# Degree one-hots as whole-block bf16 operations in a graph and mixture-of-experts layer

## The chip, the cores and the metric

One Trainium2 chip, one of its cores. The metric is the device time of one execution, in microseconds (us). PE is TensorE (PEld its weight loads), DVE is VectorE, ACT is ScalarE, POOL is GpSimd, SP is SyncE, which here only starts transfers.

## The reference, cut to what matters

One layer over 6250 nodes of 256 numbers and 100,000 edges sorted by target. It has a graph convolution, a linear attention and a mixture of 16 experts, two per node. The part around the change is the degree of each node, its inverse root, and the normalised rows that the edges gather:

```python
def gcn_residual(x, edge_index, edge_weight, W, b, gamma, beta):
    src, dst = (edge_index[0], edge_index[1])
    h = x @ W
    deg = jax.ops.segment_sum(edge_weight, dst, num_segments=N_NODES) + 1.0
    dinv = jax.lax.rsqrt(deg)
    norm = dinv[src] * edge_weight * dinv[dst]
    agg = jax.ops.segment_sum(norm[:, None] * h[src], dst, num_segments=N_NODES)
    agg = agg + (dinv * dinv)[:, None] * h
...
xn = _layernorm(x, axis=-1)
x = x + gcn(xn, edge_index, edge_weight, ...) + mix(xn[None], ...)[0]
x = x + ffn(_layernorm(x, axis=-1)[None], ...)[0]
```

## The kernel before

**Stages.** `gps_layer` loads the edges' targets, weights and sources as rows of 1024 (`load_rows`: targets by SP's queue, weights and sources by ACT's), and X, the nodes' rows, by SP's queue. It turns the edges' rows into columns of 128 edges by PE's transposes (`columns`, L158 to L165): `loc_t` (the target within the window of the edge's chunk), `w_t`, `src_t`. A check that the edges fit into these windows decides between two layers; `windowed_layer` is the one that runs, and all that follows is in it.

**The degree stage** (L397 to L520). There are NCH = 782 chunks of 128 edges, each with a window of 128 nodes. The degrees come from products of one-hots. A target within its window is split into its low four bits `lo_b` and its high bits `hi_b` (HI = 8 values). The weight is split into three bf16 parts (`thirds`, `w3`), whose sum has the precision of f32. DVE goes through blocks of 98, 98, 196, 196 and 196 chunks. For a block it builds `lo1`, the one-hot of the low bits, with 16 operations (L460), and `hw`, the one-hot of the high bits times each of the three weight parts, with 24 (L464). PE then makes one product per chunk (L472): 128 edges, 16 low values by 24 columns (8 high values times 3 parts), added into PSUM at the chunk's group. PSUM holds three banks, each of HB = 168 groups of three columns; a product that crosses the edge of a bank is split in two. Products with zeros open and close each bank (L454, L480). Both one-hots have two buffers, so DVE may be up to two blocks ahead of PE.

When the banks are closed, DVE adds the three parts (L506). PE spreads the 16 x groups onto partitions with eight products against `spread` (L514). ACT takes the root (L517), and DVE the reciprocal `dinv` and its product with the layer norm's inverse deviation (L518 to L520). `keep_pace` (L484) is a row of products with zeros that nobody reads.

**Beside it.** ACT sums the first SA = 32 tiles of X and their squares (`two_sums`, L441), in groups of eight; DVE takes the statistics of the other 17 with bn_stats (L498). `constants` and the splitting of two bias rows (L490, L492) also run on DVE. SP's queue loads the weights and then writes zeros over the first 88 of 129 blocks of `xslots`, the experts' input rows in device memory (`fill`, L385, eight blocks or 1 MB for each transfer; SOON = 88, L394).

**The table.** DVE and ACT write `hs`, each node's row normalised and scaled by `dinv` (`table`, L529), in groups of seven tiles that SP's queue stores (L540). `table` is called from the first 14 slots of the main loop, numbered -14 to -1.

**The main loop** (L1358) runs over slots, about one for each chunk. The order of PE, DVE, ACT and SP is written out by hand: each engine runs its instructions in the order in which the program makes them. In a slot POOL starts the gather of a chunk's 128 rows of `hs` (L1364), DVE builds the chunk's weighted one-hot (L1369), and PE multiplies (L1377). `Weave` runs pieces of other work at slots that are set beforehand: the attention (`attend`), the residual, the routing, POOL's scatter of tokens to `xslots` (L1040), the experts, whose results go to `yslots`. ACT's queue writes the rest of the zeros from slot 4 on, one transfer every eight slots, first `yslots`, then the rest of `xslots` (L1280). `own_term` (L660) loads a tile's own row of `hs` into a ring of ten buffers (`ring`, L652). The tail then gathers the experts' results (L1180) and ends the layer.

The lines L558 to L567 (half of `par`, the mask `heads`, the ones in `xa`) stand on DVE between the degree stage and the table.

Of the kernel before, what the change touches and what calls it, by code (L numbers as in the profile page):

```python
# [111 lines left out]
HB = 168  # L112
# [17 lines left out]

WA = 2 * F
# [13 lines left out]
def evicted_at(c):  # L145

    return product_at(c) + (3 if c < 16 * PHASES[-2] else 1)

# [39 lines left out]
def gps_layer(ctx: ExitStack, tc: tile.TileContext, x, src, dst, ew, **rest):  # L188
# [12 lines left out]
    flag = top.tile([1, 1], I32, name="flag")  # L201
    with tc.tile_pool(name="chk", bufs=1) as cp, \
# [4 lines left out]
        v.memset(dst_e[:, PADC:], N - 1)  # L207
        v.memset(ew_e[:, PADC:], 0.0)
# [37 lines left out]
    with tc.If(ok) as cmp:  # L246
        windowed_layer(tc, X, ident, loc_t, w_t, src_t, **rest)
# [11 lines left out]
def windowed_layer(ctx: ExitStack, tc: tile.TileContext, X, ident, loc_t, w_t, src_t, W, b, gamma, beta, wqT, wkvT, wprojT, bproj,  # L259
# [124 lines left out]

    def fill(eng, a, first, end):  # L385

        zero = zero_b.bitcast(F32)
        for s in range(first, end, 8):
            q = min(8, end - s)
            eng.dma_start(a[s * P:(s + q) * P, :].rearrange("(p q) c -> p q c", q=q),  # L390
                          zero[:, None, :].to_broadcast([P, q, D]))
            yield 8

    SOON = 88  # L394
    for _ in fill(nc.sync, xslots, 0, SOON):
        pass
    with tc.tile_pool(name="deg", bufs=1) as sp, \  # L397
            tc.tile_pool(name="deg_ps", bufs=1, space=bass.MemoryType.PSUM) as sps:
        spread = sp.tile([16, 8, P], F32, name="spread")
        nc.gpsimd.memset(spread, 0.0)  # L400
        for a in range(8):
            nc.gpsimd.tensor_copy(spread[:, a, a * 16:(a + 1) * 16], ident[:16, :16])

        rowf = sp.tile([1, NB3], F32, name="rowf")
        nc.scalar.dma_start(rowf[:, :D], b.rearrange("(p c) -> p c", p=1))
        nc.scalar.dma_start(rowf[:, D:2 * D], bproj.rearrange("(p c) -> p c", p=1))
# [3 lines left out]
        nc.scalar.dma_start(b2f, experts.rearrange("(e p) w -> e p w", p=P)[:, 0, WROW - D:])  # L410
        b2s = sp.tile([NE, 3, D], BF, name="b2s")

        loc_i = sp.tile([P, NCA], I16, name="loc_i")
        v.tensor_copy(loc_i, loc_t)
        lo_i = sp.tile([P, NCA], I16, name="lo_i")
        hi_i = sp.tile([P, NCA], I16, name="hi_i")
        v.tensor_scalar(lo_i, loc_i, 15, None, op0=OP.bitwise_and)
        v.tensor_scalar(hi_i, loc_i, 4, None, op0=OP.logical_shift_right)
        lo_b = sp.tile([P, NCA], BF, name="lo_b")
        hi_b = sp.tile([P, NCA], BF, name="hi_b")  # L420
# [3 lines left out]
        def thirds(o, a):  # L424
            left = sp.tile([P, NCA], F32, name="left", bufs=2)[:a.shape[0], :a.shape[1]]
            v.tensor_copy(o[:, 0, :], a)
            v.tensor_sub(left, a, o[:, 0, :])
            v.tensor_copy(o[:, 1, :], left)
            v.tensor_sub(left, left, o[:, 1, :])
            v.tensor_copy(o[:, 2, :], left)  # L430

        w3 = sp.tile([P, 3, NCA], BF, name="w3")
        thirds(w3, w_t)


        SA = 32
# [4 lines left out]
        def two_sums():  # L441
            for t0 in range(0, SA, 8):
                for t in range(t0, t0 + 8):
                    act(sp.tile([P, D], F32, name="unread", bufs=2), X[:, t, :], AF.Identity,
                        accum_out=sums_[:, t:t + 1])
                act(minus[:, t0:t0 + 8], sums_[:, t0:t0 + 8], AF.Identity, scale=-1.0 / D)
                for t in range(t0, t0 + 8):
                    act(sp.tile([P, D], F32, name="unread", bufs=2), X[:, t, :], AF.Square,
                        bias=minus[:, t:t + 1], accum_out=squares[:, t:t + 1])


        deg = sps.tile([16, 3, 512], F32, name="deg")
        for i in range(3):
            nc.tensor.matmul(deg[:, i, :3 * HB], zero_b[:, :16], zero_b[:, :3 * HB], start=True, stop=False)  # L454
        C = NCA // 4
        c0 = 0
        for n in (C // 2, C // 2, C, C, C):
            lo1 = sp.tile([P, 16, C], BF, name="lo1", bufs=2)
            for i in range(16):
                v.tensor_scalar(lo1[:, i, :n], lo_b[:, c0:c0 + n], float(i), None, op0=OP.is_equal)  # L460
            hw = sp.tile([P, HI, 3, C], BF, name="hw", bufs=2)
            for i in range(HI):
                for s in range(3):
                    v.scalar_tensor_tensor(hw[:, i, s, :n], hi_b[:, c0:c0 + n], float(i), w3[:, s, c0:c0 + n],  # L464
                                           op0=OP.is_equal, op1=OP.mult)
            for c in range(c0, min(c0 + n, NCH)):
                g0 = 4 * group_of(c)
                h0 = g0
                while h0 < g0 + HI:
                    i = h0 // HB  # L470
                    h1 = min(g0 + HI, (i + 1) * HB)
                    nc.tensor.matmul(deg[:, i, (h0 - i * HB) * 3:(h1 - i * HB) * 3], lo1[:, :, c - c0],  # L472
                                     hw[:, h0 - g0:h1 - g0, :, c - c0].rearrange("p h s -> p (h s)"),
                                     start=False, stop=False)
                    h0 = h1
            if c0 == 0:
                two_sums()
            c0 += n
        for i in range(3):
            nc.tensor.matmul(deg[:, i, :3 * HB], zero_b[:, :16], zero_b[:, :3 * HB], start=False, stop=True)  # L480

# [8 lines left out]
        thirds(row3, rowf)  # L490
        nc.sync.dma_start(bias3, row3)
        thirds(b2s, b2f)  # L492
# [8 lines left out]
        v.bn_aggr(mv1[:rows(NFULL), NFULL, :], halves[NFULL][:rows(NFULL)])  # L501
        v.tensor_scalar(mv1[:, :SA, 0], minus, -1.0, None, op0=OP.mult)
        v.tensor_scalar(mv1[:, :SA, 1], squares, 1.0 / D, None, op0=OP.mult)
        deg16 = sp.tile([16, 3, HB], F32, name="deg16")
        for i in range(3):
            v.tensor_reduce(deg16[:, i, :], deg[:, i, :3 * HB].rearrange("p (h s) -> p h s", s=3),  # L506
                            axis=AX.X, op=OP.add)
        inv_std(sp, rs1, mv1[:, :, 1])
        minus_mean(nm1, mv1, rs1)

        dps = sps.tile([P, NT], F32, name="dps")
        d8 = deg16.rearrange("p i h -> p (i h)")[:, 4:4 + 8 * NT].rearrange("p (t a) -> p t a", a=8)
        for a in range(8):
            nc.tensor.matmul(dps, spread[:, a, :], d8[:, :, a], start=(a == 0), stop=(a == 7))  # L514
        keep_pace(10)
        sdeg = sp.tile([P, NT], F32, name="sdeg")
        act(sdeg, dps, AF.Sqrt, bias=ones[:, 0:1], scale=1.0)  # L517
        v.reciprocal(dinv, sdeg)  # L518
# [39 lines left out]
    v.tensor_scalar(par, par, 0.5, None, op0=OP.mult)  # L558
    heads = part(P)
    v.memset(heads, 0.0)  # L560
    for h in range(P // HEAD):
        v.memset(heads[h * HEAD:(h + 1) * HEAD, h * HEAD:(h + 1) * HEAD], 1.0)
    XA = 6
    xa = []
    for i in range(XA):
        xa.append(part(D + 1))
        v.memset(xa[i][:, D:], 1.0)  # L567
# [82 lines left out]
    RING = 10  # L650
    hTs = [wp.tile([P, F], F32, name=f"hT{j}") for j in range(2)]
    ring = [wp.tile([P, D], F32, name=f"agg{j}") for j in range(RING)]  # L652
# [627 lines left out]
    for a, first in (yslots, 0), (xslots, SOON):  # L1280
# [77 lines left out]
    while slot <= evicted_at(NCH - 1) or weave.steps:  # L1358
        for t in range(NT * (slot + PRE) // PRE, NT * (slot + PRE + 1) // PRE if slot < 0 else 0):
            table(t)  # L1360
# [554 lines left out]
```

## Time and profile before

| | us |
|---|---|
| median of 11 runs | 1465.18 |
| lowest and highest run | 1461.02, 1468.98 |
| the profiled execution | 1470.76 |
| its span, first to last instruction | 1469.0 |
| first one-hot of the degree stage | 21.09 |
| last bank closed | 71.42 |
| table begins | 79.72 |
| first gather | 106.81 |
| last gather issued | 1206.70 |

The profile is one execution, taken by the hardware profiler. The page gives each engine's busy time and share of the span, and groups of instructions: source line, engine, operation, output<-input by the program's names, shape, count, busy us, mean ns of one, then the idle time of the engine just before them and what ended it. A timeline lists instructions in order of time: start, length, engine, line, and in brackets the idle time before and who ended it. Matmuls are pipelined and their ends are modelled, so the distance between starts says more than a single length. An f32 matmul shows as two records. The granted clock is the share of TensorE's full speed that the throttle left, 0.931 over the whole span. Busy shares of the span are PE 83%, PEld 67%, POOL 65%, DVE 62%, ACT 34%.

### The profile page before, as it was taken

What the parts mean: (1) busy time and instruction counts of PE and PEld (TensorE: products, weight loads), DVE (VectorE), ACT (ScalarE), POOL (GpSimd) and SP (SyncE); (2) the same over time, 40 slices, a digit from 0 to 9 for tenths busy, and PEclk for the clock granted to TensorE, in tenths of its full rate; (3) what the DMA queues carried; (4) which work ended last, traced back from release to release, by engine and by line L of the source; (5) the groups of instructions that cost most, each with busy time, mean ns of one, the idle gap of its engine ahead of it and who ended that gap; (6) DMA issues with size and microseconds to landing.
All of it is one profiled execution on the core that took longest, in us unless ns stands there. A gap on an engine that the chain in (4) does not pass through costs nothing. (4 is left out here: it accounts for less than half of the span.)

```text
span 1469.0 us, 24398 instructions
## 1 busy us (share of the span) xinstructions
PE 1216.7 (83%) x6927; PEld 989.0 (67%) x6927; DVE 914.5 (62%) x3303; ACT 501.4 (34%) x1428; POOL 962.1 (65%) x998
## 2 busy tenths in 40 slices
PE   4889999978837897989968899797986999878880
PEld 3846666656625786868857787586875887767670
DVE  7954444449958583855837568286582657657764
ACT  6464444412202221322322223132231233446772
POOL 1007777777777777777777777777777763157732
PEclk9999999989967998989989999898998999989995
DMA  8976666763334777877868877687877886899983
GB/s 260 312 236 219 188 216 206 223 216 105 104 118 163 247 229 227 273 260 246 278 203 297 268 230 270 220 280 245 278 249 263 308 300 206 296 332 388 383 298 86
DMA packets 180593, 357.20 MB, mean 243 GB/s; under 512 B 27157, under 2 KB 119692, under 8 KB 180442
## 3 DMA queue, kind: packets, MB, share of 16 engines
q1 hardware_dynamic: 110334, 204.18, 40.4%
q0 software_dynamic: 47712, 128.17, 27.8%
q10 hardware_dynamic: 22396, 23.10, 4.8%
q8 instruction: 61, 1.00, 0.3%
q14 instruction: 90, 0.74, 0.2%
HBM read 279.28 MB, written 76.06 MB: 242 GB/s over the span
## 5 line engine op out<-in xcount | busy, mean ns | idle before, releaser
L1364 POOL DMA_INDIRECT hrow<-w_hs,src_t x782 | 758.6, 970 | 325.1 <-issue 88.1
L1377 PE MATMUL acc<-hrow,hot 128*128 128x256 f32 x1564 | 448.4, 405 | 105.0 <-DMA hrow<-w_hs,src_t 94.4
L1377 PEld LDWEIGHTS acc<-hrow,hot 128*128 128x128 f32 x1564 | 282.4, 200 | 182.7 <-issue 89.4
L1369 DVE TENSOR_SCALAR hot<-iota_g,loc_t,w_t 128x128 f32<-128x128 f32 x782 | 247.2, 354 | 65.3 <-PE acc L1377 64.4
L1129 ACT ACTIVATE hT<-hp,early 128x128 f32<-128x128 f32 x292 | 83.2, 369 | 256.0 <-PE hp L1122 134.1
L1133 PE MATMUL yp<-early,hT 128*128 128x256 f32 x584 | 143.8, 391 | 0.4 <-ACT hT L1129 0.4
L1122 PE MATMUL hp<-Q,early 128*128 128x128 f32 x992 | 124.5, 280 | 3.9 <-ACT Q L1116 3.9
L1122 PEld LDWEIGHTS hp<-Q,early 128*128 128x128 f32 x992 | 122.7, 197 | 7.4 <-ACT Q L1116 4.9
L1133 PEld LDWEIGHTS yp<-early,hT 128*128 128x128 f32 x584 | 114.2, 198 | 16.9 <-ACT hT L1129 0.5
L1040 POOL DMA_INDIRECT w_xslots<-Q,slot_i x92 | 91.6, 996 | 40.2 <-issue 32.0
L1122 PE MATMUL hp<-Q 128*128 128x128 f32 x832 | 104.8, 280 | 12.1 <-ACT Q L1116 12.0
L1122 PEld LDWEIGHTS hp<-Q 128*128 128x128 f32 x832 | 102.3, 196 | 15.8 <-ACT Q L1116 13.8
L1386 DVE SCALAR_TENSOR_TENSOR agg<-acc,dinv,agg 64x256 f32<-64x256 f32 x135 | 65.1, 482 | 70.5 <-PE acc L1377 68.0
L588 PE MATMUL kq<-early,xnT 128*128 128x512 f32 (+1 forms) x196 | 94.3, 604 | 6.3 <-ACT xnT L584 6.3
L1133 PE MATMUL yp<-Q,hT 128*128 128x256 f32 x328 | 86.1, 409 | 5.0 <-ACT hT L1129 5.0
L596 DVE SCALAR_TENSOR_TENSOR row<-two_a,two_b 128x256 f32<-128x256 f32 (+1 forms) x49 | 20.9, 426 | 103.4 <-ACT two_b L593 103.4
L1180 POOL DMA_INDIRECT late<-w_yslots,slot_i x48 | 48.6, 1012 | 49.6 <-DVE xn L1208 20.0
L1129 ACT ACTIVATE hT<-hp,Q 128x128 f32<-128x128 f32 x164 | 46.7, 370 | 93.7 <-issue 44.1
L1133 PEld LDWEIGHTS yp<-Q,hT 128*128 128x128 f32 x328 | 66.5, 208 | 16.3 <-ACT hT L1129 6.2
L1180 POOL DMA_INDIRECT agg<-w_yslots,slot_i x50 | 50.7, 1013 | 22.5 <-DVE xn L1195 6.3
L1111 PE MATMUL xtp<-ident,Q 128*128 128x128 f32 x228 | 46.2, 285 | 22.9 <-DMA Q<-w_xslots 21.5
L1116 ACT COPY Q<-xtp 128x256 f32<-128x256 f32 x114 | 43.1, 378 | 54.9 <-PE xtp L1111 54.6
(322 smaller groups left out, 1765.5 us busy)
## 6 DMA issues: line engine op xcount, KB each, us to landing
early<-in_experts SPq DMA_DIRECT2D x60, 642.0 KB
early<-in_experts SPq DMA_DIRECT2D x62, 512.0 KB
Q<-in_experts SPq DMA_DIRECT2D x52, 512.0 KB
Q<-in_experts SPq DMA_DIRECT2D x28, 642.0 KB
w_yslots<-zero_b ACTq DMA_DIRECT2D x16, 1024.0 KB
Q<-w_xslots SPq DMA_DIRECT2D x114, 128.0 KB
w_yslots<-Q SPq DMA_DIRECT2D x114, 128.0 KB
hrow<-w_hs,src_t POOLq DMA_INDIRECT x782
```

The costliest lines, as they stand in the source:

```text
L588: nc.tensor.matmul(kq[:r], xnT[:, k, :r], wkq[:, k, :], start=(k == 0), stop=(k == 1))
L1040: i = nc.gpsimd.indirect_dma_start(out=xslots, out_offset=IndirectOffsetOnAxis(ap=slot_i[:r, t, k:k + 1], axis=0), in_=y[:r], in_offset=No ...
L1111: nc.tensor.transpose(tp[:, c, :], xs[:, c * P:(c + 1) * P], ident)
L1116: nc.scalar.copy(xT, tp[:, :2, :])
L1122: nc.tensor.matmul(hp[:, f, :], w1[:, c, f * P:(f + 1) * P], xT[:, c, :], start=(c == 0), stop=(c == 1))
L1129: act(hT[:, f, :], hp[:, f, :], AF.Relu, bias=b1[:, f:f + 1], scale=1.0)
L1133: nc.tensor.matmul(yp[:, :D], hT[:, f, :], w2[:, f, :], start=(f == 0), stop=(f == FJ - 1 and not as_row))
L1180: g = nc.gpsimd.indirect_dma_start(out=got[i, k]()[:r], out_offset=None, in_=yslots, in_offset=IndirectOffsetOnAxis(ap=slot_i[:r, t, k:k + ...
L1364: nc.gpsimd.indirect_dma_start(out=hrows[c], out_offset=None, in_=hs, in_offset=IndirectOffsetOnAxis(ap=src_t[:, c:c + 1], axis=0))
L1369: v.tensor_scalar(hots[c], iota_g[:, group_of(c) % 2, :], loc_t[:, c:c + 1], w_t[:, c:c + 1], op0=OP.is_equal, op1=OP.mult)
L1377: nc.tensor.matmul(accs[g], hots.pop(c), hrows.pop(c), start=begin, stop=end)
L1386: v.scalar_tensor_tensor(agg(t)[p0:p1], acc[p0:p1, :], dinv[p0:p1, t:t + 1], agg(t)[p0:p1], op0=OP.mult, op1=OP.add)
```

## The change

It does five things.

1. Each one-hot block is built with five operations in place of 40. A constant `which` holds the numbers 0 to 15, each repeated over a block's columns, in bf16; it lies in `turns`, memory that is later the first seven buffers of the ring, and is written by 16 memsets at the very beginning of `gps_layer`. `lo1` is one comparison of `which` with the broadcast `lo_b`, `hi1` another with `hi_b`, and `hw` is three products of `hi1` with the weight's parts.
2. Two chunks go into one degree product: even and odd chunks stand apart (`by_parity`), and a product has 32 columns of weights (16 values x 2) by 48 moving columns (8 x 3 x 2). Of its result only the parts with equal parity are read. A bank holds 84 groups instead of 168, so there are five banks. `spread` and its products are doubled to 16.
3. A bank is closed as soon as no later chunk falls into it, and its parts are added before the next block of one-hots is built; what is left is added at the end.
4. SP's queue writes 40 blocks of zeros before the main loop instead of 88. ACT's queue writes the rest in the loop, `xslots` first.
5. Other moves. ACT sums 36 tiles in groups of twelve, and its sums now stand ahead of the blocks in the program. The splitting of the bias rows goes from DVE to POOL, and their loads from ACT's queue to SP's. `heads` and the ones in `xa` are set by POOL ahead of the degree stage, and `par` is halved in slot -1. The reciprocal of the first deviation comes behind the spread's products.

```diff
-HB = 168
+HB = 84
+PAIR = 2
...
+RING = 10
...
+def numbers(turns):
+
+    n = NCA // 4
+    return turns.rearrange("p a c -> p (a c)").bitcast(BF)[:, :16 * n].rearrange("p (i n) -> p i n", i=16)
...
         v.memset(dst_e[:, PADC:], N - 1)
+        for i in range(16):
+            bits = int(np.array([i], np.float32).view(np.uint32)[0]) >> 16
+            v.memset(numbers(turns).bitcast(I32)[:, i, :], bits << 16 | bits)
         v.memset(ew_e[:, PADC:], 0.0)
         v.memset(src_e[:, PADC:], 0)
...
+    def halve():
+        v.tensor_scalar(par, par, 0.5, None, op0=OP.mult)
+
+    heads = part(P)
+    nc.gpsimd.memset(heads, 0.0)
...
-    SOON = 88
-    for _ in fill(nc.sync, xslots, 0, SOON):
-        pass
+    SOON = 40
...
+        def by_parity(a):
+            return a.rearrange("p (q j) -> p j q", j=PAIR)
...
+        v.tensor_copy(loc_i, by_parity(loc_t))
...
-        SA = 32
+        SA, SG = 36, 12
...
+        def cell(i, h0, h1):
+            return deg[:, i, 3 * PAIR * h0:3 * PAIR * h1]
+
+        def whole(i, start):
+            nc.tensor.matmul(deg[:, i, :PAIR * 3 * HB], zero_b[:, :R2], zero_b[:, :PAIR * 3 * HB],
+                             start=start, stop=not start)
...
+        def add_thirds(i):
+            for j in range(PAIR):
+                v.tensor_reduce(deg16[:, j, i, :], cell(i, 0, HB).rearrange("p (h s j) -> p j h s", s=3, j=PAIR)[:, j, :, :],
+                                axis=AX.X, op=OP.add)
+
+        two_sums()
         for n in (C // 2, C // 2, C, C, C):
-            lo1 = sp.tile([P, 16, C], BF, name="lo1", bufs=2)
-            for i in range(16):
-                v.tensor_scalar(lo1[:, i, :n], lo_b[:, c0:c0 + n], float(i), None, op0=OP.is_equal)
-            hw = sp.tile([P, HI, 3, C], BF, name="hw", bufs=2)
-            for i in range(HI):
-                for s in range(3):
-                    v.scalar_tensor_tensor(hw[:, i, s, :n], hi_b[:, c0:c0 + n], float(i), w3[:, s, c0:c0 + n],
-                                           op0=OP.is_equal, op1=OP.mult)
-            for c in range(c0, min(c0 + n, NCH)):
+            while added < full:
+                add_thirds(added)
+                added += 1
+            m, q0 = n // PAIR, c0 // PAIR
+
+            def same(name, k, key):
+                o = sp.tile([P, k, PAIR, CP], BF, name=name, bufs=2)
+                v.tensor_tensor(o[:, :, :, :m], which[:, :k, :, :m],
+                                key[:, None, :, q0:q0 + m].to_broadcast([P, k, PAIR, m]), op=OP.is_equal)
+                return o
+
+            lo1, hi1 = same("lo1", 16, lo_b), same("hi1", HI, hi_b)
+            hw = sp.tile([P, HI, 3, PAIR, CP], BF, name="hw", bufs=2)
+            for k in range(3):
+                v.tensor_tensor(hw[:, :, k, :, :m], hi1[:, :, :, :m],
+                                w3[k][:, None, :, q0:q0 + m].to_broadcast([P, HI, PAIR, m]), op=OP.mult)
+            for c in range(c0, min(c0 + n, NCH), PAIR):
+                q = (c - c0) // PAIR
                 g0 = 4 * group_of(c)
+                while full < g0 // HB:
+                    whole(full, False)
+                    full += 1
...
-                    nc.tensor.matmul(deg[:, i, (h0 - i * HB) * 3:(h1 - i * HB) * 3], lo1[:, :, c - c0],
-                                     hw[:, h0 - g0:h1 - g0, :, c - c0].rearrange("p h s -> p (h s)"),
+                    nc.tensor.matmul(cell(i, h0 - i * HB, h1 - i * HB), lo1[:, :, :, q].rearrange("p i j -> p (i j)"),
+                                     hw[:, h0 - g0:h1 - g0, :, :, q].rearrange("p h s j -> p (h s j)"),
                                      start=False, stop=False)
...
-        thirds(row3, rowf)
+        thirds(nc.gpsimd, [row3[:, k, :] for k in range(3)], rowf)
...
+        while added < NBANK:
+            add_thirds(added)
+            added += 1
...
-        for a in range(8):
-            nc.tensor.matmul(dps, spread[:, a, :], d8[:, :, a], start=(a == 0), stop=(a == 7))
+        for j in range(PAIR):
+            d8 = deg16[:, j, :, :].rearrange("p i h -> p (i h)")[:, 4:4 + 8 * NT].rearrange("p (t a) -> p t a", a=8)
+            for a in range(8):
+                nc.tensor.matmul(dps, spread[:, j, a, :], d8[:, :, a], start=(j == 0 and a == 0), stop=(j == PAIR - 1 and a == 7))
...
-    ring = [wp.tile([P, D], F32, name=f"agg{j}") for j in range(RING)]
+    ring = [turns[:, j, :] for j in range(RING - 3)] + [wp.tile([P, D], F32, name=f"agg{j}") for j in range(3)]
...
-    for a, first in (yslots, 0), (xslots, SOON):
+    for a, first in (xslots, SOON), (yslots, 0):
...
+        if slot == -1:
+            halve()
```

## The prediction

> **What bounds the kernel now.** First the page's costliest groups, and a window over the main stage (the second one, ahead of it, comes up below), for what sets its length.
>
> ```profile
> L1364 POOL DMA_INDIRECT hrow<-w_hs,src_t x782 | 758.6, 970 | 325.1 <-issue 88.1
> 107.00:1207.00 1100.00, 948.83 (x4836) 767.54 (x4836) 668.94 (x2387) 305.99 (x797) 837.67 (x862) 0.93 0.70 231
> 70.00:82.00 12.00, 11.52 (x40) 5.90 (x38) 7.78 (x44) 5.37 (x10) 0.00 (x0) 1.00 0.00 1
> ```
>
> (A window's columns: its ends, its length, busy us and instructions of PE, PE's weight loads, DVE, ACT and POOL, the granted clock, DMA's share, GB/s.)
>
> In those 1100 us POOL issues 862 times, one in 1.276 us: 0.97 busy, 0.30 between issues. PE is at 86% and DMA at 0.70, and the pace of POOL does not change with either. So the main stage has a fixed length, and a move of the first gather moves the end by as much. Then the timeline ahead of that gather, engine by engine (start, length, both us).
>
> ```profile
> 106.81 1.23 POOL L1364 DMA_INDIRECT hrow<-w_hs,src_t  x1 [87.19 <-DMA hT<-w_hs]
> ...
> 40.94 24.05 PE L472 MATMUL deg<-hw,lo 128*16 128x24 bf16 x506 [3.62 <-DVE hw L464]
> 65.35 4.80 PE L472 MATMUL deg<-hw,lo 128*16 128x24 bf16 x96 [0.37 <-issue]
> 69.98 1.44 PE L480 MATMUL deg<-zero_b 128*16 128x504 bf16 x3
> 71.21 1.91 PE L486 MATMUL idle<-zero_b 128*16 128x512 bf16 x4
> 73.46 3.62 PE L514 MATMUL dps<-deg,spread 16*128 16x49 f32 x16 [0.33 <-DVE deg L506]
> ...
> 21.09 1.60 DVE L460 TENSOR_SCALAR lo<-lo_b 128x98 bf16<-128x98 bf16 x16
> 22.61 4.18 DVE L464 SCALAR_TENSOR_TENSOR hw<-hi_b,w 128x98 bf16<-128x98 bf16 x24
> ...
> 32.33 2.01 DVE L460 TENSOR_SCALAR lo<-lo_b 128x196 bf16<-128x196 bf16 x16
> 34.26 6.63 DVE L464 SCALAR_TENSOR_TENSOR hw<-hi_b,w 128x196 bf16<-128x196 bf16 x24
> 50.75 2.02 DVE L460 TENSOR_SCALAR lo<-lo_b 128x196 bf16<-128x196 bf16 x16 [1.40 <-PE deg L472]
> 71.46 1.85 DVE L506 TENSOR_REDUCE deg<-deg 16x168 f32<-16x504 f32 x3 [0.29 <-PE deg L480]
> 79.72 8.49 DVE L534 TENSOR_SCALAR Q<-X,mv,rsd 128x256 f32<-128x256 f32 x26
> ```
>
> The reader is to see: from 40.94 on PE multiplies without a pause up to the closing of the banks at 71.42, while DVE runs ahead of it, by two blocks, and builds under PE's cover. From 71.42 the path is serial: additions, spread, root, reciprocal, table at 79.72, its stores, gathers. The window from 70 to 82 us has a DMA share of 0.00, and from 82 to 104, under the stores, it is 0.98: the table's start moves the gathers one for one, and no zero fill is in the way of it.
>
> How long is one degree product, and what would a wider one be? PE's timeline again, in two short windows, and the forms of four DVE rows from the groups of the first 160 us.
>
> ```profile
> 47.11 0.66 PE L472 MATMUL deg<-hw,lo 128*16 128x12 bf16 x15
> 47.82 1.00 PE L472 MATMUL deg<-hw,lo 128*16 128x24 bf16 x17
> L426 DVE CAST w<-w_t 128x784 bf16<-128x784 f32 x1 | 0.6, 554 | 0.0
> L421 DVE CAST lo_b<-lo_i 128x784 bf16<-128x784 int16 x1 | 0.3, 345 | 0.0
> L427 DVE TENSOR_TENSOR left<-w_t,w 128x784 f32<-128x784 f32 x1 | 1.0, 985 | 0.0
> SPq L214 <- DMA rows<-in_ew: 3.4, 1, 3.4
> ```
>
> Fifteen products of 12 columns: (0.66 - 0.18 for the last one's own length)/14 = 34 ns apart. Seventeen of 24: (1.00 - 0.23)/16 = 48 ns. The time follows the columns, so these products are no fixed cost. The contiguous 512 columns of L486 go at about 0.82 ns a column (4.43 us for ten, their own 0.63 off, by nine); here a column, read with a stride of a whole block, takes 2 ns.
>
> **The change, part by part.** Sums go against this execution, 1470.76 us with a span of 1469.0; the runs' median is 1465.18, and the difference is carried over to it.
>
> *One-hots.* 200 small operations become 5 x 5 large ones. A block of n columns holds 16n + 8n + 3 x 8n = 48n elements per partition. No row shows a bf16 TENSOR_TENSOR. Bounds: one per cycle as L464 (from 98 to 196 columns it grows by 0.102 us, 1.04 ns a column), four as L460 (0.26 ns). I take two, 0.52 ns: between the two casts the halved input doubles the rate (0.554 to 0.345 us, of which about 0.14 is fixed), and L427 in f32 is one per cycle. With 0.1 us per operation a block of 98 takes 2.95 us (5.7 before), of 196 5.4 us (8.6).
> The Trainium skill, "VectorE: DVE Perf Modes", section "The perf-mode tier table (the rule you actually need)", gives tensor_tensor in bf16 two per cycle; against it stands the row L464, two bf16 inputs at one. By the rule the sum is the one below, by that row it is rival C's; no run here shows which.
>
> *Products.* 784 of 16 x 24 become 392 of 32 x 48, some split at a bank's edge. Bounds: 48 ns (as now) and 96 (twice both operands). 34 to 48 ns for 12 more columns gives 1.2 ns each, so 78 at least if the rest stays; 2 ns a column gives 96, and a load of 32 strided columns instead of 16 (twice the 34 ns) lies under it. I take 96. So halving their number buys PE nothing.
> The Trainium skill, "TensorE: Matmul & The Clock Gate", section "Part 1: The HAM clock gate (the "warmup" mystery)", has start to start at N / 1.2 GHz while the array is cold: 40 ns for 48 columns, and 20 for 24, where the trace has 48. By the rule it would be rival B's sum; the trace decides against it.
>
> *Banks read as they fill.* This adds a wait. DVE's additions of a bank stand ahead of the next block's one-hots, and in the order of the changed program the last two banks' four additions share one wait: it is for all products issued so far, not for the bank. So DVE stops until PE has finished the block, and PE then stops until DVE has built the next; before, DVE ran ahead. Queued behind the waiting addition are the one-hots, and PE waits for these. With T the first one-hot: block 2's products end at T + 13.4 (49 x 0.096 + 0.2 behind the first build and hand-over at 3.1, then 45 x 0.096, 8 halves at 0.065, a closing 0.42, 0.2). Each later round: two additions 0.66 (L506: 0.59 for 504, so 0.33 for 252), build 5.4, hand-overs 0.2, 94 x 0.096 = 9.0, halves 0.5, closing and drain 0.6: 16.4. Three rounds and one closing more: T + 62.9. Before it was 71.42 - 21.09 = 50.3. **+12.6.**
>
> *Start T.* Sixteen memsets of 128x98 (L323, same form: 140 ns; L207, 0.37 us for 352, gives 0.10 each) stand on DVE ahead of the memsets that release ACT's loads of weights and sources: these go 1.6 us later, behind X's first load. The last row of the fence shows X's second load held by the weights until now; it will go sooner and be ahead of the sources, which ACT casts at 11.79. 0 to +3; I take 1.0. The strided reads by parity (three operations of 784): 0 to 1.8 by L938, a strided read of 128 that takes 384 ns where L862 has 286; I take 0.5. **+1.5.**
>
> *Behind the last product.* Four additions (1.4) lie under the four idle products (1.7): 1.7 to the spread instead of 2.04: **-0.35**. The spread has 16 products for 8, by L514 0.40 each: **+3.2**. Moved off DVE from between root and table (L558, 560, 562, 567, from 78.31 to 79.57): **-1.26**. halve() now stands between the last tables, 0.42, part of it under stores: **+0.2**.
>
> *At nothing.* The thirds of the biases (59.85 to 64.18) go to POOL, idle from 19.6 to 106.8; bn_stats of 13 tiles (17 before, 0.40 each) ends before PE's last block does; ACT's 36 tiles at 0.9 us each (0.40 and 0.49) end near 49, sooner than anything waits. Without that cover each is worth its length: 4.3, 5.2, up to 5. SP's five fills instead of eleven (2.9 us each to issue, from about 35) end before 52; the bias stores and the table's stores queue behind them, and none is due then. ACT's queue gets six fills more (0.54 us each) from about slot 4 to 236; in the window above DMA is at 0.70 and POOL's pace held with such fills (102 to 320 us).
>
> Sum: 12.6 + 1.5 - 0.35 + 3.2 - 1.26 + 0.2 = **+15.9 us**, 1486.7 for the profiled execution, **1481.1** for the median.
>
> **Rivals.** *B, products at 48 ns.* For it: half as many, same instruction count a piece. Against: 34 and 48. Block 2 then ends at T + 9.1, a round is 11.7, the end T + 44.6: -5.7 in place of +12.6, so -2.4: 1462.8. It decides below about 55 ns a product, and with T unmoved (-3.9) it is faster.
> *C, one-hots at one per cycle* (for it L464, against it the casts): each large build 4.9 us longer, small 2.4, and all of it on the path since the rounds are serial: +34, 1499.
> *D, faster:* one-hots at four per cycle and products at 48: builds of 3 us, -11: 1454. For it L460; against it that L460 reads one tensor.
> That the wait holds only for the bank (then about +8) lies in the range.
>
> **How the numbers follow.** Forecast 0.62, B 0.17, C 0.11, D 0.10. About 0.2% (2.9 us) is what a measurement can tell from no change. Forecast: 0.61 slower, 0.01 the same; B 0.11 the same, 0.06 faster; C slower; D faster. So 0.16 faster, 0.12 the same, 0.72 slower. The forecast's own range is 78 ns with T unmoved (+7) to T at its upper bounds with slower additions (+21 to +25): 1472 to 1490. Reaching to B gives 1462 to 1490; C and D lie outside.
>
> **What would show it.** Right: PE's degree products about 96 ns apart, in four or five bursts of some 10 us with 6 us of idle before each, "<-DVE hw"; DVE idle about 10 us before each bank's addition, "<-PE deg"; the first gather near 123 instead of 106.8; POOL's pace still 1.28. Wrong: products near 50 ns; a build of 196 columns of 10 us or 3 us; additions that start while PE is in the middle of a block; the first gather moved and the end not.

## The result, and the profile after

The changed kernel takes 1486.28 us (median of 12 runs, 1480.04 to 1489.85); the kernel before took 1466.3 beside it (46 runs). The ratio is 1.0132, 95% interval 1.0118 to 1.0147: 17 to 22 us slower. The forecast was 1481.1, in a range of 1462 to 1490. The profiled execution has a span of 1482.7 us and took 1484.6.

First the page's costliest group, then the timeline of the changed kernel (start, length, both us), engine by engine. In its lines L525 are the one-hots, L532 the weight products, L513 the additions, L544 the degree products, L504 the products that close a bank, L583 the spread, L606 the table, L1427 the gathers.

```profile
L1427 POOL DMA_INDIRECT hrow<-w_hs,src_t x782 | 754.5, 965 | 315.1 <-issue 100.8
```

```profile
124.31 1.16 POOL L1427 DMA_INDIRECT hrow<-w_hs,src_t  x1 [77.23 <-DMA hT<-w_hs]
...
36.99 1.57 PE L544 MATMUL deg<-hw,lo 128*32 128x48 bf16 x16
46.33 6.21 PE L544 MATMUL deg<-hw,lo 128*32 128x48 bf16 x72 [7.77 <-DVE hw L532]
52.38 0.58 PE L504 MATMUL deg<-zero_b 128*32 128x504 bf16 x1
52.76 2.83 PE L544 MATMUL deg<-hw,lo 128*32 128x48 bf16 x30
61.77 4.91 PE L544 MATMUL deg<-hw,lo 128*32 128x48 bf16 x58 [6.19 <-DVE hw L532]
...
86.05 0.60 PE L504 MATMUL deg<-zero_b 128*32 128x504 bf16 x1
86.45 1.91 PE L557 MATMUL idle<-zero_b 128*16 128x512 bf16 x4
88.29 7.06 PE L583 MATMUL dps<-deg,spread 32*128 32x49 f32 x32
...
26.26 0.98 DVE L525 TENSOR_TENSOR lo<-turns,lo_b 128x1568 bf16<-128x1568 bf16 x1
...
42.02 4.26 DVE L532 TENSOR_TENSOR hw<-hi,w 128x1568 bf16<-128x1568 bf16 x3
55.62 0.73 DVE L513 TENSOR_REDUCE deg<-deg 32x84 f32<-32x252 f32 x2 [9.34 <-PE deg L544]
56.28 1.77 DVE L525 TENSOR_TENSOR lo<-turns,lo_b 128x3136 bf16<-128x3136 bf16 x1
57.98 0.96 DVE L525 TENSOR_TENSOR hi<-turns,hi_b 128x1568 bf16<-128x1568 bf16 x1
58.97 2.75 DVE L532 TENSOR_TENSOR hw<-hi,w 128x1568 bf16<-128x1568 bf16 x3
...
95.72 0.47 DVE L590 RECIPROCAL dinv<-sdeg 128x49 f32<-128x49 f32 x1 [5.02 <-ACT sdeg L587]
...
96.71 0.41 DVE L606 TENSOR_SCALAR Q<-X,mv,rsd 128x256 f32<-128x256 f32 x1
```

The picture is the predicted one. VectorE (DVE) waits 9.34 us for TensorE (PE), adds two rows, builds for 5.4 us (56.28 to 61.72); meanwhile PE waits 6.19 us for it. The products go 6.21/72 = 86 ns apart. The gathers have their old pace: 965 ns each, 970 before, and, without the long wait ahead of the first one (77.23 and 87.19 us), 0.30 us idle between two in both. They start at 124.31 instead of 106.81. So the loss is all ahead of them: 17.5 us. (From the first to the last gather it is 1095.2 us, 1099.9 before. The profiled spans differ by 13.7 only, the medians by 20.0; single executions of either kernel scatter over 10 us.)

The way to VectorE's first table operation, 79.72 before and 96.71 after, splits into five terms, each the difference of two pairs of rows. (ScalarE's first one, beside it, starts at 78.56 before and 96.83 after.) The row of `dinv` before:

```profile
77.44 0.47 DVE L518 RECIPROCAL dinv<-sdeg 128x49 f32<-128x49 f32 x1 [3.52 <-ACT sdeg L517]
```

| from | to | before | after | difference |
|---|---|---|---|---|
| start | first one-hot | 21.09 | 26.26 | +5.17 |
| first one-hot | last bank closed | 50.33 | 60.39 | +10.06 |
| last bank closed | first spreading product | 2.04 | 1.64 | -0.40 |
| first spreading product | dinv | 3.98 | 7.43 | +3.45 |
| dinv | first table operation | 2.28 | 0.99 | -1.29 |

The first term was forecast at 1.5. What became late in it, on ScalarE (ACT), DVE and GpSimd (POOL), first before, then after; ACT's column copy of loc_t was at 8.54 before:

```profile
15.67 1.25 DVE L418 TENSOR_SCALAR hi_i<-loc_i 128x784 int16<-128x784 int16 x1
15.68 1.02 POOL L400 MEMSET spread<- 16x1024 f32 x1
```

```profile
10.60 0.23 ACTq L165 DMA_DIRECT2D rows<-in_src  x1
10.86 1.28 ACT L238 ACT_TABLE_LOAD   x1 [10.86 <-DMA rows<-in_ew]
...
12.25 1.57 ACT L175 COPY loc_t<-tpe 128x392 f32<-128x392 f32 x2
...
19.94 2.09 DVE L456 TENSOR_SCALAR hi_i<-loc_i 128x784 int16<-128x784 int16 x1
...
19.94 1.86 POOL L425 MEMSET spread<- 32x2048 f32 x1
```

ACT issues the loads of weights and sources from 3.40 instead of 1.65 us. The last of them is stuck on ACT's queue until 10.60 (5.04 before), and the table load and the copies are queued behind it.

### The profile page after: what moved, and what is told of

It reads as the page before. It is cut to its first block, busy times and chain, and to the rows that moved or that the text cites. A ratio compares the mean times of both kernels' runs of the same rounds, so it can differ in the third digit from the quotient of the medians.

```text
span 1482.7 us, 23524 instructions
## 1 busy us (share of the span) xinstructions
PE 1220.6 (82%) x6556; PEld 993.1 (67%) x6556; DVE 898.4 (61%) x3122; ACT 504.7 (34%) x1443; POOL 975.9 (66%) x1027
## 5 line engine op out<-in xcount | busy, mean ns | idle before, releaser
L1427 POOL DMA_INDIRECT hrow<-w_hs,src_t x782 | 754.5, 965 | 315.1 <-issue 100.8
L1449 DVE SCALAR_TENSOR_TENSOR turns<-acc,dinv,turns 64x256 f32<-64x256 f32 (+2 forms) x99 | 47.8, 482 | 52.3 <-PE acc L1440 50.3
L654 ACT ACTIVATE two_a<-kq 128x512 f32<-128x512 f32 (+1 forms) x49 | 29.2, 596 | 89.2 <-PE kq L650 68.2
```

The source lines that it names most:

```text
L1427: nc.gpsimd.indirect_dma_start(out=hrows[c], out_offset=None, in_=hs, in_offset=IndirectOffsetOnAxis(ap=src_t[:, c:c + 1], axis=0))
L1449: v.scalar_tensor_tensor(agg(t)[p0:p1], acc[p0:p1, :], dinv[p0:p1, t:t + 1], agg(t)[p0:p1], op0=OP.mult, op1=OP.add)
```

## The experiments

The twelve runs were made in three groups on three chips. On two of these every kernel is longer (the kernel before takes 1700.82 and 1686.83 us), so each ratio is to runs of the kernel before on the same chip. What is longer is the main stage: the changed kernel once more, control_after, needs 1274 us from the first to the last gather there instead of 1095, at a granted clock of 0.89 instead of 0.93, while its stages up to the table lie within 0.7 us of the first execution's. thirds_dve, single_last and best_k32 were run once and have no ratio. All numbers but the ratio are us in the profiled execution:

| run | first one-hot | last bank closed | spread takes | first table op (DVE) | first gather | ratio (95%) |
|---|---|---|---|---|---|---|
| before | 21.09 | 71.42 | 3.62 | 79.72 | 106.81 | |
| after | 26.26 | 86.65 | 7.06 | 96.71 | 124.31 | 1.0132 (1.0118-1.0147) |
| control_after | 26.94 | 86.76 | 7.06 | 96.82 | 123.99 | 1.0088 (1.0056-1.0119) |
| adds_last | 26.32 | 68.98 | 5.32 | 78.94 | 106.13 | 1.0003 (0.9984-1.0023) |
| adds_behind | 26.66 | 71.63 | 4.09 | 78.66 | 106.21 | 1.0018 (1.0003-1.0032) |
| bank_tiles | 26.58 | 78.62 | 7.06 | 88.68 | 116.72 | 1.0101 (1.0069-1.0133) |
| memsets_behind | 22.63 | 82.97 | 7.06 | 93.02 | 120.27 | 1.0074 (1.0053-1.0096) |
| thirds_dve | 26.33 | 85.21 | 3.95 | 92.16 | 119.04 | |
| single_last | 26.18 | 70.93 | 3.61 | 78.01 | 105.13 | |
| fills | 21.96 | 71.76 | 3.62 | 80.19 | 107.14 | 1.0008 (0.9986-1.0029) |
| qmajor_last | 22.61 | 55.98 | 7.03 | 68.26 | 95.74 | 0.9940 (0.9922-0.9958) |
| repaired | 22.29 | 63.03 | 7.06 | 73.08 | 100.83 | 0.9959 (0.9944-0.9973) |
| best | 21.22 | 49.90 | 2.97 | 59.62 | 87.51 | 0.9884 (0.9863-0.9906) |
| best_k32 | 22.13 | 50.84 | 5.28 | 59.65 | 87.19 | |

**Where the additions stand: adds_last, adds_behind.** adds_last leaves out the additions between the builds (they all run at the end); adds_behind has them behind the next build instead:

```
-            while added < full:
-                add_thirds(added)
-                added += 1
             m, q0 = n // PAIR, c0 // PAIR
             ...
+            while added < full:          (adds_behind only)
+                add_thirds(added)
+                added += 1
             for c in range(c0, min(c0 + n, NCH), PAIR):
```

> The changed kernel with the additions of all five banks behind the last build, none between two builds. Theory: an addition in front of a build waits for the last product of the block before it, so builds and products take turns, and TensorE stands idle some 6 us ahead of each of the three large blocks. Without it the products follow one another: their bursts in the changed kernel sum to 35.8 us and the bank products between them to some 2, so from the first product at 29.4 us the last bank is closed at about 68 us instead of 86.65; five additions instead of two are then left (+2.2 us), and the first table operation falls from 97.0 to about 80 us, the time from 1486 to about 1469 us (1465 to 1474). Rival 1, the builds and the products disturb each other when they run side by side: pace over 96 ns, last bank closed after 72 us. Rival 2, the additions' place is not what costs: time at 1482 us or more, idle time ahead of the large blocks still near 6 us.

> The changed kernel with each bank's addition moved behind the next block's build instead of in front of it; banks are still read as they fill. Theory (the wait for the whole block is harmless once the next block's one-hots are already there): last bank closed near 68 us as with all additions at the end, but only two banks left to add behind it, so the first table operation is near 78 us and the time near 1467 us (1463 to 1472). Rival, the addition only moves the turn by one block and the build behind it comes too late again: idle time of 3 us or more ahead of some large block, last bank closed after 73 us, time above 1473 us.

PE's timeline of adds_last:

```profile
41.37 6.20 PE L541 MATMUL deg<-hw,lo 128*32 128x48 bf16 x72 [2.75 <-DVE hw L529]
47.42 0.58 PE L504 MATMUL deg<-zero_b 128*32 128x504 bf16 x1
47.79 7.57 PE L541 MATMUL deg<-hw,lo 128*32 128x48 bf16 x88
55.21 0.58 PE L504 MATMUL deg<-zero_b 128*32 128x504 bf16 x1
55.58 7.57 PE L541 MATMUL deg<-hw,lo 128*32 128x48 bf16 x88
```

From 41.37 on PE works without a pause, at the same 86 ns (7.57/88), and the last bank is closed 17.7 us sooner. That is the theory; both rivals fall. The early additions, meant to save 2 us at the end, had cost 18. In adds_behind the expected 68 became 71.63, between the theory and its rival:

```profile
42.04 6.21 PE L544 MATMUL deg<-hw,lo 128*32 128x48 bf16 x72 [3.08 <-DVE deg L513]
```

PE still waits 3.08 us ahead of the third block (the rival's sign), most of it for the build, as in adds_last (2.75), the rest for the addition behind it; and 0.82 us ahead of the two others, for the addition itself. It adds less at the end (1.4 us instead of 3.5), and the first gather lies where adds_last has it.

**What the additions wait for: bank_tiles.** Five tiles instead of one of five banks:

```
-        deg = sps.tile([R2, NBANK, 512], F32, name="deg")
+        deg = [sps.tile([R2, 512], F32, name=f"deg{i}") for i in range(NBANK)]
```

> The changed kernel with its five banks as five tiles instead of one tile of five banks; nothing else. Theory: the addition of a bank waits for the block's last product, not for the bank's closing product, because both stand in one tile. By the changed kernel's trace the closing product of the first three banks ends 1.4, 2.6 and 3.8 us ahead of the products that the additions waited for, so the last bank is closed some 7.8 us earlier (near 79 us instead of 86.65), and the first table operation comes near 89 us, the time is some 8 us less than the changed kernel's (about 0.5% over before). Rival: the additions still wait for the block, last bank closed at 86 to 87 us; then the wait's grain lies elsewhere (a count of TensorE that is raised once in a block).

DVE's timeline of bank_tiles; the releaser is what ended the wait:

```profile
51.40 0.73 DVE L513 TENSOR_REDUCE deg<-deg 32x84 f32<-32x252 f32 x2 [6.72 <-PE deg L504]
```

The addition now waits for the closing product (L504), which ends at 51.36, and no longer for the block's last (L544). The last bank is closed 8.0 us earlier, the first gather comes 7.6 earlier. So the wait for the whole block came from the tile: the order is kept tile by tile, and five banks in one tile are one thing. The waiting as such stays (3.57 us of PE ahead of the fourth block).

**What the number table costs: memsets_behind.** The sixteen fills stand behind the two that the loads wait for:

```
-        for i in range(16): ... v.memset(numbers(turns) ...)
         v.memset(ew_e[:, PADC:], 0.0)
         v.memset(src_e[:, PADC:], 0)
+        for i in range(16): ... v.memset(numbers(turns) ...)
```

> The changed kernel with its sixteen fills of the number table put behind the two small fills that the loads of weights and sources wait for. Theory: the loads' issue at 3.40 instead of 1.65 us puts them behind the six loads of X, and that alone moves the degree stage's start: zero_b from 18.80 back to about 14.7 us, the first one-hot from 26.26 to about 22.1 us, the first table operation from 97.0 to about 93, the time from 1486 to about 1482 us (1479 to 1485). Rival, the loads' delay is only the 1.8 us of the fills themselves: first one-hot near 24.5 us, time 1484 us. Rival, the delay comes from elsewhere: nothing moves.

ACT's timeline of memsets_behind:

```profile
4.98 0.27 ACTq L165 DMA_DIRECT2D rows<-in_src  x1
5.27 1.28 ACT L238 ACT_TABLE_LOAD   x1 [5.27 <-DMA rows<-in_src]
...
8.49 1.58 ACT L175 COPY loc_t<-tpe 128x392 f32<-128x392 f32 x2 [1.74 <-PE tpe L174]
```

ACT's loads and its first copy are back at their old place, and the first one-hot comes 3.63 us earlier than in the changed kernel; 1.54 us behind the kernel before remain, 0.84 of them `hi_i`. So a delay of 1.75 us at the issue had become 3.6 on the path: the fills' own length is no measure of what they cost. That this is so because the loads then stood behind more of X is read off the order of issue; no run moves X, so it is not shown.

**GpSimd beside VectorE: thirds_dve.**

```
-        thirds(nc.gpsimd, [row3[:, k, :] for k in range(3)], rowf)
+        thirds(v, [row3[:, k, :] for k in range(3)], rowf)
```

(and so for b2s).

> The changed kernel with the bias thirds back on VectorE, GpSimd without them. Theory: GpSimd's thirds slow the third block's weight products on VectorE; alone these take 2.75 us (fourth block) instead of 4.26, the third build ends some 1.5 us earlier and the last bank is closed some 1.5 us earlier relative to the first one-hot (58.9 instead of 60.4 us). Rival: the 4.26 us have another cause (the first use of a buffer, products of TensorE beside it) and stay. The thirds themselves should cost nothing on VectorE as long as they fit in the 3.9 us between its last statistics and the closing of the last bank.

The third block's weight products on DVE, and the spread on PE, in thirds_dve:

```profile
42.09 2.75 DVE L532 TENSOR_TENSOR hw<-hi,w 128x1568 bf16<-128x1568 bf16 x3
...
86.85 3.95 PE L583 MATMUL dps<-deg,spread 32*128 32x49 f32 x32
```

2.75 instead of 4.26, and the last bank closed 1.44 us earlier. In the changed kernel POOL's operations beside them were stretched as well:

```profile
39.11 3.14 POOL L471 CAST b2s<-left 16x256 bf16<-16x256 f32 x1
42.22 1.87 POOL L472 TENSOR_TENSOR left<-left,row 1x512 f32<-1x512 f32 x1
```

In best, where they run behind DVE's builds, the same two take 0.39 and 1.15 us:

```profile
54.14 0.39 POOL L467 CAST b2s<-left 16x256 bf16<-16x256 f32 x1
54.51 1.15 POOL L468 TENSOR_TENSOR left<-left,row 1x512 f32<-1x512 f32 x1
```

`hi_i` is the same case: it ends 0.2 us behind POOL's fill of `spread` in each trace, 2.09 us beside a fill of 1.86, 1.23 beside one of 1.01 (best). The Trainium skill, "SBUF — State Buffer", section "SBUF: two separate sides", says that GpSimd shares a pair of ports with those VectorE instructions that read two operands from SBUF or run in a mode that uses both ports, and that whichever starts first holds the pair to its end while the other stands still; the rows of the weight products and the thirds agree. That `hi_i`, which reads one operand, runs in such a mode is not shown here. The further 3.1 us between the banks and the table were not expected: the spread took 3.95 instead of 7.06 us (last section).

**What pairing buys: single_last.** `HB = 168`, `PAIR = 1` in adds_last.

> The kernel with all additions at the end, and one chunk to a product (16 x 24 instead of 32 x 48; three banks of 168 instead of five of 84; eight spreading products instead of sixteen). Theory: pairing saves little, since a product's time goes with the columns it reads: 798 products at the 48 ns that the kernel before shows for 24 columns are 38.3 us, against 407 at 86 ns, 35.0 us; last bank closed near 71 us instead of 68.98, three additions instead of five (-1.4 us) and eight products less to spread (-1.3 to -2.7 us), so the first table operation comes within 2 us of the 78.7 us with pairs. Rival, pairing is worth what halving the number of products suggests: pace over 80 ns for single chunks too, last bank closed after 95 us.

PE's timeline: the longest stretch of single products.

```profile
48.16 16.46 PE L541 MATMUL deg<-hw,lo 128*16 128x24 bf16 x344
```

48 ns for 24 columns, 798 of them 38 us against 35 for 407 pairs. PE saves 2 us, and the spread and the additions give 3 back (more, had adds_last's spread not run half its passes at the full clock, last section): with single chunks the first gather comes 1.0 us earlier. Pairing two chunks buys nothing at this layout.

**Why a product takes 86 ns: qmajor_last.** In adds_last, the one-hots are stored product by product; the number table is 16 x 2, filled behind the loads' fills:

```
-                o = sp.tile([P, k, PAIR, CP], BF, name=name, bufs=2)
+                o = sp.tile([P, CP, k, PAIR], BF, name=name, bufs=2)
...
-            hw = sp.tile([P, HI, 3, PAIR, CP], BF, name="hw", bufs=2)
+            hw = sp.tile([P, CP, HI, 3, PAIR], BF, name="hw", bufs=2)
...
-                 lo1[:, :, :, q].rearrange("p i j -> p (i j)"),
+                 lo1[:, q, :, :].rearrange("p i j -> p (i j)"),
```

> The kernel with all additions at the end, and the one-hots laid out product by product, so that TensorE reads the 32 and 48 columns of a product side by side instead of 196 bytes apart; VectorE then writes them in runs of two numbers, and the number table shrinks from 16 x 196 to 16 x 2 numbers, filled behind the loads' small fills. Theory: the 86 ns of a product are the price of the strided reading; side by side the pace falls to 50 ns or less (24 strided columns took 48), the products' 35 us to some 20, and if VectorE keeps its 2 elements a cycle in runs of two (1.77 us for a first-key one-hot of a whole block) the stage is bound by the builds: last bank closed near 52 us, first table operation near 62 us, time some 17 us below before. Rival 1, VectorE falls to one element a cycle (3.3 us for the same one-hot): builds 10.5 us a block, last bank closed near 68 us, table near 77 us, time 2 to 3 us below before. Rival 2, the pace stays near 86 ns whatever the layout: last bank closed near 65 us.

PE's, then DVE's timeline of qmajor_last, the third block:

```profile
35.01 2.93 PE L540 MATMUL deg<-hw,lo 128*32 128x48 bf16 x72 [3.34 <-DVE hw L528]
37.78 0.58 PE L503 MATMUL deg<-zero_b 128*32 128x504 bf16 x1
38.15 1.19 PE L540 MATMUL deg<-hw,lo 128*32 128x48 bf16 x30
...
28.89 1.78 DVE L521 TENSOR_TENSOR lo<-turns,lo_b 128x3136 bf16<-128x3136 bf16 x1
30.58 0.98 DVE L521 TENSOR_TENSOR hi<-turns,hi_b 128x1568 bf16<-128x1568 bf16 x1
31.60 3.35 DVE L528 TENSOR_TENSOR hw<-hi,w 128x1568 bf16<-128x1568 bf16 x3
```

The same product takes 2.93/72 = 41 ns when its columns lie side by side: the stride was half its price, and PE now waits for DVE. A clock twice as fast would do the same, but it is not that: the closing product of 504 contiguous columns stands 0.37 us ahead of the next product here (37.78 to 38.15) and 0.38 in the changed kernel (52.38 to 52.76). The edit lays the 32 columns of weights side by side as well as the 48 that are multiplied, and no run separates the two. But with the weights strided as they were, the halves at a bank's edge, of 24 columns, start 54 ns apart in the changed kernel's trace and whole products 87: 33 ns for 24 columns, so most of the price goes with the multiplied columns. DVE writes runs of two numbers as fast as long ones (1.78 us, 1.77 in the changed kernel); only the weight products, which leave gaps, lose something (3.35 for 2.75). The last bank is closed at 55.98 (expected 52; POOL's thirds stretch the later builds), and with additions of 3.5 and a spread of 7.0 us behind it the kernel is 0.6% faster than before.

**The fills alone: fills.** The kernel before with `SOON = 40` and the two tables' order swapped.

> The kernel before with the change's zero fills alone: 40 instead of 88 blocks of the first table in front, the rest ahead of the second table's beside the attention. Theory: nothing waits for them; first table operation at 79.6 us as before, time within 0.2% of before. Rival, they are on a path: 1 us or more either way.

1.0008, an interval around 1: no effect that can be measured.

**Putting it together: repaired, best, best_k32.** repaired joins adds_behind, bank_tiles, memsets_behind and thirds_dve and keeps the strided layout. best joins qmajor_last and bank_tiles, with

```
         two_sums()
+        nc.scalar.dma_start(rowf[:, :D], ...)       (and the other biases: from SP to here)
...
+        while added < NBANK - 2: add_thirds(added); added += 1
         for t in range(SA, NT):
+            if t == SA + 6: (the last two banks' additions)
...
-        deg16 = sp.tile([R2, PAIR, NBANK, HB], F32, name="deg16")
+        deg16 = sp.tile([PAIR * 32, NBANK, HB], F32, name="deg16")
-                v.tensor_reduce(deg16[:, j, i, :], ...
+                v.tensor_reduce(deg16[32 * j:32 * j + 32, i, :], ...
```

and best_k32 is best without the last two edits. control_after is the changed kernel once more.

> The changed kernel as it is, beside the other three that run with it. First one-hot at 26.3 us, last bank closed at 86.7, time 1.2 to 1.5% over before.

> The changed kernel with its strided layout kept and three of its costs taken out: the additions behind the next build and each bank a tile of its own, the number table filled behind the loads' small fills, the bias thirds on VectorE. Theory, the costs are separate and add up: first one-hot at 22.6 us, TensorE then held up by its own 86 ns a product (35.0 us and 2 for the closing products, with one wait of some 1 us ahead of the third block), last bank closed near 64 us, two additions, spreading of 4 to 7 us by TensorE's pace at that moment, first table operation between 70.5 and 74 us against 79.7 before; time 0.4 to 0.6% below before. Rival, a wait comes in their place (a one-hot buffer that the products hold): last bank closed after 68 us, time within 0.2% of before or above it.

> The product-by-product layout with everything learnt: each bank a tile, the first three additions behind the last build and the last two among the statistics, the biases loaded behind the statistics of ScalarE so that GpSimd's thirds run after the builds, and the two halves of a bank's sums on different partitions, so that eight spreading products do instead of sixteen and GpSimd's zero fill of their table is half as long (1.0 us). Theory: VectorE is the bound from the first one-hot on. First one-hot near 21.8 us (the shift beside the shorter fill 1.25 instead of 2.09 us), builds 3.1 us for a half block and 6.1 for a whole one (no thirds beside them), products closed near 52 us, spreading some 3.6 us, first table operation near 58.5 us against 79.7 before; time 1.2 to 1.6% below before. Rival, the main stage doesn't start with the table any more (a load or a weight is late): the first gather more than 28 us behind the first table operation, time less than 1% below before.

> The same with sixteen spreading products of 32 rows. Theory: spreading takes 7.0 instead of 3.6 us at the slow pace, GpSimd's zero fill 1.86 instead of 1.0 us and with it the shift 2.09 instead of 1.25 us: first table operation some 3 to 4 us later than with eight products. Rival: the statistics that VectorE still has to do behind the last addition cover the spreading, and the table moves by 1 us or less.

control_after has its stages where they were expected, but its time is 0.9% over before (0.6 to 1.2), not 1.2 to 1.5: 15.6 us in the medians, for 17.2 at the first gather. repaired came out as the sum: closed at 63.03, first table operation at 73.08, ratio 0.9959. So the costs are separate, and without them even the strided version beats the kernel before. best closes its last bank sooner than expected (49.90), starts its table at 59.62 instead of 58.5, and is 1.2% faster than before, the least that was expected. DVE's timeline of best, last build and what follows, then PE's spread:

```profile
42.09 3.38 DVE L528 TENSOR_TENSOR hw<-hi,w 128x1568 bf16<-128x1568 bf16 x3
...
57.53 0.47 DVE L587 RECIPROCAL rs<-sd 128x49 f32<-128x49 f32 x1 [1.74 <-ACT sd L349]
...
59.62 0.73 DVE L605 TENSOR_SCALAR Q<-X,mv,rsd 128x256 f32<-128x256 f32 x2 [0.41 <-DMA w_b2rows<-b2s]
...
52.69 2.97 PE L582 MATMUL dps<-deg,spread 64*128 64x49 f32 x16 [1.82 <-DVE deg L509]
```

The root of the statistics, not the spread, is waited for last (1.74 us), and the late thirds hold the table by 0.41. That is why best_k32, where sixteen spreading products take 5.28 us, starts its table at the same time (59.65): its rival was right and the theory wrong.

## Why the prediction was right, and where it was off

- *The main stage has a fixed length and the first gather moves the end.* Held: 17.5 us at the gather go with 17 to 22 in time. In every run with a ratio the difference of the medians is within some 3 us of that at the gather (-11.1 us at the gather and -10.2 in the medians for qmajor_last, -19.3 and -20.1 for best; the widest are +9.9 and +12.9 in bank_tiles, -0.6 and +2.5 in adds_behind).
- *Banks read as they fill, +12.6.* The mechanism was right in each part: one wait for all that was issued so far, turns of PE and DVE, 6 us of idle PE. Its size was 10.06. In it the product was priced at 96 ns and took 86 (407 products by 10 ns are 4.1 us); against that stand the 1.5 us of GpSimd's thirds. That a wait for the bank alone would leave "about +8" was somewhat low: +9.9 at the gather and +12.9 in the medians in bank_tiles.
- *A column costs by its stride; pairing buys PE nothing.* Held, by qmajor_last and single_last. The prediction weighed the rule of the Trainium skill, "TensorE: Matmul & The Clock Gate", section "Part 1: The HAM clock gate (the "warmup" mystery)", of N / 1.2 GHz and let the trace decide against it. For strided columns that stands (86 ns, not 40); side by side it is met (41 ns). Rival B's price of a product would have been right with another layout; its sum, with the additions still in front of the builds, was not run.
- *One-hots at two a cycle.* Held: 0.98 us for 1568 and 1.77 for 3136 elements are 0.50 ns for each further element, against the 1.04 that the prediction took from L464 for one a cycle. Rivals C and D fall.
- *Start T, +1.5.* This step failed: 5.17. The loads behind X were taken at 1.0 in bounds of 0 to 3 and cost 3.6 (memsets_behind). The strided reads, taken at 0.5, cost 0.1 (`loc_i` 0.61 for 0.52). POOL's longer fill of `spread` beside `hi_i`, 0.84, was in no term. The 0.6 that remain are no more than the scatter: the same start gives a first one-hot at 21.09 in before and 21.96 in fills.
- *At nothing: the thirds on an idle POOL.* This failed too: POOL was idle, but its operations and DVE's hold each other up, 1.5 us (thirds_dve). The statistics and ACT's longer share did cost nothing (they end at 82.8 and 52.6 us, the last bank closes at 86.65), nor did the fills, by the run of that name.
- *Spread +3.2, idle products -0.35, operations moved away -1.26.* Measured +3.45, -0.40, -1.29. The first is of this size because both spreads ran at half the clock; in thirds_dve the same sixteen products took 0.3 us more than the eight before, not 3.4 (last section). halve() and all else between the table's start and the first gather, taken at +0.2, came to +0.5.

The errors were of both signs: T 3.7 more, the banks 2.5 less. That the sum of 15.9 lies close to the 17.5 at the gather is partly luck.

## What to carry to other kernels

Reading a result early pays only if the reader's queue holds nothing that the producer needs next: put the read behind the next block's work, and give each part that is read alone a tile of its own. Before narrowing or widening a product, look at how its columns lie; here the layout halved the time of a product, while pairing saved PE 2 us and lost them again behind it. And an engine that is idle is not free cover: look at what its operations share with the engine they are to relieve.

## What the runs showed that was not expected

The same 32 passes of the spread took 7.03 to 7.06 us in six runs and 3.95, 4.09, 5.28 and 5.32 in four others. The granted clock decides it: it is either 1.00 or 0.50, and it changed in the middle of some spreads. Two windows of adds_last, on either side of the change at 74.14 us (columns as in the prediction, PE's count first):

```profile
72.40:74.00 1.60, 1.60 (x16) 1.60 (x16) 0.22 (x3) 1.30 (x2) 0.00 (x0) 1.00 0.05 10
74.60:76.20 1.60, 1.60 (x9) 1.60 (x9) 0.43 (x2) 0.00 (x0) 0.00 (x0) 0.50 0.00 0
```

By their starts, the passes of these ten runs go 112 ns apart at 1.00 and 213 at 0.50. The records of the clock begin late in each trace, and a window ahead of them reads 1.00 whatever the pace. So it is in the changed kernel, whose first record lies at 98.15 us:

```profile
88.30:95.30 7.00, 7.00 (x34) 6.91 (x34) 0.68 (x2) 1.62 (x2) 0.00 (x0) 1.00 0.01 2
```

Its passes go 213 ns apart, as at 0.50, and the products of 512 columns behind them turn from 427 to 217 ns where the records begin. The records start whole multiples of 3.41 us apart (in best at 46.58, 49.99 and 53.40). The Trainium skill, "TensorE: Matmul & The Clock Gate", section "Part 1: The HAM clock gate (the "warmup" mystery)", has the array's clock double after a busy window of some 3.4 us that runs freely; the traces agree in the factor and in the length. Where a spread falls among these windows differs from run to run; what makes a window count as busy is not shown here. What it means for the accounts above: up to 3 us of a table's start can come from this and not from an edit (thirds_dve, adds_behind). The closing of the last bank is free of it in every run with strided products, since there the first record lies behind it; in qmajor_last, best and best_k32 the clock already changes during the blocks, where PE waits for DVE.

Why the main stage is longer on two of the three chips stays open.
